# Attention on one core: the accumulator as two one-bank tiles, two second halves one place later, and copies of g and of the sums dealt anew between ScalarE and VectorE

## The chip, the cores and the metric

The kernel runs on one core of a Trainium2 chip. The metric is the device time of one execution in microseconds. Three runs of the kernel before took 578.69, 578.71 and 579.06 us; their median is 578.71 us.

A core has a matrix engine (TensorE, "PE" in the profile, with its weight loads as "PEld"), a vector engine (VectorE, "DVE"), a scalar engine (ScalarE, "ACT"), GpSimd ("POOL"), and a synchronisation engine (SyncE, "SP"). Each engine takes its instructions in the order in which the program issued them. Matmuls write to PSUM; here a PSUM bank is a tile of 128 partitions by 512 float32 columns. VectorE and ScalarE read PSUM and write to SBUF, where all operands of a matmul lie.

## The reference

Two graph layers work on x (16 batches, 1024 nodes, 64 channels) with one matrix adj (1024 x 1024). What matters here:

```
Q = x Wq^T + bq;  K = x Wk^T + bk;  V = x Wv^T
score = softmax(Q K^T, axis=1)           # over the first node index
x = layernorm(x + (score @ adj) @ V)     # adj is (1024, 1024) here too
# second layer: x, adj x, 2 adj (adj x) - x, for each of two equal supports,
# concatenated, times a weight, plus a bias
x = layernorm(x + that)
```

Everything is float32. The kernel computes Q K^T as x G x^T with one 64 x 64 matrix G (g2 in the code) and one bias vector gb. It keeps g = G x + gb, transposed (GT in the code), as one side of the scores, and the transposed x (xT) as the other.

## The kernel before

**Pairs and steps.** Two batches form a pair, one on partitions 0 to 63 and one on 64 to 127 of the transposed tiles. The loop at line 678 runs over pairs p = 0 to 7, and inside it over steps m = 0 to 7, one for each block of 128 nodes. A step computes the scores of the *next* step for both batches (j = 0 and 1) in two halves of 512 columns (h = 0 and 1), their maxima (`nm`, line 398, VectorE) and exponentials (`e`, line 400, ScalarE, which also yields the sums `es`). It then scales rows of U by the reciprocals of the sums (`scaled`, lines 403 to 413, giving `us`) and multiplies: `weighted` (line 415) adds us times e into the accumulator ACC[p], over all eight steps. In the code `weighted(p, m, t, h)` takes the node half t, which is a row half of TensorE, and the column half h. The part t = 0 runs in the step itself, t = 1 in the step after.

**Tiles of TensorE.** Every matmul of the loop uses 64 rows and 64 columns of the array, so four can run side by side. The program alternates between rows 0 to 63 (j = 0 or t = 0) and rows 64 to 127 (j = 1 or t = 1). A float32 matmul is issued twice, so each appears twice in the counts of the profile.

**Runs.** Beside the attention, U = adj x (first layer) and a product for the second layer are computed by a seven-product scheme in blocks, in pieces called runs (class Run, line 653). Each step carries one run, six steps two (`two_runs`, line 605). A run has four parts, part(t, i), and is then evicted from PSUM by VectorE by a small program of additions (`Hop.evict`, line 280): "u=" copies, "+p" adds the product to a destination, "u+p" to the tile u, and "+u" adds u to a destination, all in SBUF.

**Small products.** Some steps carry a small product as well (`small_of`, line 633). At m=1 it is `values` of the pair before, which multiplies the attended rows OT by the value weights and adds to x. At m=4 it is `project`, which makes GT for the next pair. At m = 7, 0, 2 and 3 it is `mix` of an earlier pair, which feeds the second layer. Each comes in two halves, j=0 and j=1, through one PSUM bank: the two run and small tiles f0 and f1 take turns, and a small product takes the bank that the last run left (`f_other`). The second half can only start when VectorE and ScalarE have taken the first out of the bank. In `project` (line 340) a half is copied to GT in two pieces b = 0 and 1, which lie on partitions 0 to 63 and 64 to 127 of the bank. Lines 359 to 362 deal the pieces: of the four copies ScalarE has three (line 366) and VectorE one (line 370), the second piece of the first half.

**End of a pair.** The first step of pair p (m=0) finishes the accumulator of pair q = p-1. After `weighted(..., 1, 0)`, `attended(q, 0)` copies its columns 0 to 511 to OT on ScalarE (line 437). After `weighted(..., 1, 1)`, `attended(q, 1)` copies columns 512 to 1023. ACC[p] is one tile of two banks (line 418) in a pool with one buffer.

**Order.** The schedule is written out by hand. Other VectorE work is attached to steps as jobs (`first_gap`, lines 607 to 631): sums for the runs, means and centring of x, a normalisation, transposes whose results go through DRAM by GpSimd's DMA queue, and weights of the second layer. They run after the first exponential of the step is issued. In steps with two runs the first run is evicted before the second maximum is taken (lines 738 to 745). After the loop, line 753 on, the second layer is finished; it begins with a tile `wide` in the accumulator's place (line 978). Ahead of the loop, the same place holds `pv` (line 571), evicted at once at line 577.

Of the kernel before, what the change touches and what calls it, by code (L numbers as in the profile page):

```python
# [26 lines left out]
def gnn_kernel(  # L27
# [126 lines left out]
    def mix_weights():  # L154
        nc.vector.tensor_add(w24, w1s[:, 2], w1s[:, 4])
        nc.vector.tensor_scalar(w3[:, 0], w24, 2.0, None, op0=ALU.mult)
        nc.vector.tensor_add(w3[:, 1], w1s[:, 1], w1s[:, 3])
        nc.vector.tensor_sub(w3[:, 2], w1s[:, 0], w24)
        for j in range(2):
            nc.vector.tensor_add(w3[half[j], 2], w3[half[j], 2], ident[half[j], half[j]])  # L160
# [72 lines left out]
    class Hop:  # L233
# [45 lines left out]

        def evict(self, po, n, group, copy=nc.vector.tensor_copy):  # L280
            po = po[:, 0 : len(group) * Q].rearrange("p (g q f) -> p g q f", q=2, f=P)
            u = self.u[:, group[0] : group[-1] + 1].rearrange("p g (q f) -> p g q f", q=2)
            for op in self.todo[n].split():
                if op == "u=":
                    copy(u, po)
                elif op == "u+p":
                    nc.vector.tensor_tensor(u, po, u, ALU.add)
                else:
                    d = self.d(int(op[0]), int(op[1]), group)
                    x, y = {"=": (po, u), "+p": (po, d), "+u": (u, d)}[op[2:]]  # L290
                    nc.vector.tensor_tensor(d, x, y, ALU.add)

# [10 lines left out]
    def by_place(t):  # L303
        return t.rearrange("c (a k n) -> c a k n", k=K8, a=A4)

    def rows(p):
# [33 lines left out]
    def project(p, js, pq):  # L340


        if 0 in js:
            GT[p] = att.tile([P, N], FP, tag="GT", name="GT")

        def made():
            for b in range(2):
                for j, t in zip(js, pq):
                    nc.tensor.matmul(  # L349
                        t[half[b]], g2[half[j], half[j]], xT(p)[half[j], ts(b, H)],  # L350
                        start=True, stop=True,
                    )

        def places(vector):
            for j, t in zip(js, pq):
                for b in range(2):


                    if vector == ((j, b) == (0, 1) if len(js) == 1 else j == 1):
                        g = by_block(GT[p])[half[j], 2 * b : 2 * b + 2]  # L360
                        q = t[half[b]].rearrange("c (a k n) -> c a k n", a=2, k=K8)
                        yield g, q, gb[half[b]]

        def by_scalar():
            for g, q, bias_ in places(False):
                nc.scalar.activation(g, q, AF.Identity, bias=bias_)

        def by_vector():
            for g, q, bias_ in places(True):
                nc.vector.tensor_scalar(g, q, bias_, None, op0=ALU.add)  # L370
        return (made,), by_scalar, by_vector
# [12 lines left out]
    def scores(sc, p, m, j, h):  # L384

        for c in range(2):
            nc.tensor.matmul(  # L387
                sc[half[c], ts(h, H)], GT[p][half[j], m * P + c * C : m * P + (c + 1) * C],
                xT(p)[half[j], ts(h, H)], start=True, stop=True,
            )  # L390

    def exps(p, m, j, sc):

        if j == 0:
            PU[p, m] = ([], small.tile([P, 2], FP, tag="es", name="es"))
        es, sm = PU[p, m]
        nm = small.tile([P, 1], FP, tag="nm", name="nm")
        nc.vector.tensor_reduce(nm, sc, AX.X, ALU.max, negate=True)  # L398
        e = att.tile([P, N], FP, tag="e", name="e", bufs=4)
        nc.scalar.activation(e, sc, AF.Exp, bias=nm, accum_out=sm[:, j : j + 1])  # L400
        es.append(e)
# [13 lines left out]
    def weighted(p, m, t, h):  # L415

        if (m, t, h) == (0, 0, 0):
            ACC[p] = pacc.tile([P, N], FP, tag="acc", name="acc")
        es, us = PU[p, m]
        made = [  # L420
            nc.tensor.matmul(  # L421
                ACC[p][half[j], ts(h, H)], us[half[t], j], es[j][half[t], ts(h, H)],
                start=m == 0 and t == 0, stop=m == K8 - 1, skip_group_check=True,
# [7 lines left out]

    def attended(p, h):

        if h == 0:
            OT[p] = att.tile([P, N], FP, tag="oT", name="oT", bufs=1)
        a = slice(2 * h, 2 * h + 2)
        nc.scalar.activation(by_block(OT[p])[:, a], by_place(ACC[p])[:, a], AF.Copy)  # L437

    def values(p, js, po):


        def made(ks):
            for k in ks:
                for t in range(2):
                    for j, o in zip(js, po):
                        n = k * P + t * C
                        nc.tensor.matmul(  # L447
# [122 lines left out]
    sums_of_adj(3)  # L570
    pv = pacc.tile([P, N], FP, tag="acc", name="pv")
    hop_0.product(pv, 4, (0, 1), False)
    for do in both(project, 0):
        do()
    sums_of_adj(2)
    hop_0.product(pv[:, H:], 4, (2, 3), False)
    hop_0.evict(pv, 4, ALL)
    sc = [sc_tile(f"sc{j}") for j in range(2)]
# [3 lines left out]
    for j in range(2):  # L582
        exps(0, 0, j, sc[j])

# [27 lines left out]
    at(second_gap, (0, 0), lambda: transposed(1, xT(1)))  # L612
    at(first_gap, (0, 1), sums_of_adj, 1)
    at(first_gap, (0, 2), sums_of_adj, 4)
    at(first_gap, (0, 3), mix_weights)
    at(first_gap, (0, 4), value_weights)
    for step, n in ((1, 0), 1), ((2, 0), 2), ((2, 5), 3), ((3, 0), 4):
        at(first_gap, step, hop_1.sums, n)
    at(first_gap, (1, 0), centred, w3)
    for step, n in ((HP + 1, 5), 1), ((HP + 2, 0), 2), ((HP + 2, 7), 3), ((NP - 1, 0), 4):  # L620
        at(first_gap, step, hop_z.sums, n)
    for p in range(NP):

        at(first_gap, {2: (2, 1), 6: (4, 5)}.get(p, (p, 5)), means, p)
        at(first_gap, {6: (5, 6)}.get(p, (p, 6)), centre, p)
        if p + 1 < NP:
# [12 lines left out]
    SYNC = mybir.DependencyInfo(mybir.DependencyClass.Sync, mybir.DependencyReason.DATA)  # L639
    sum_mark = []  # L640

    def passed(made):
# [10 lines left out]
    class Run:  # L653
# [13 lines left out]
        def evict(self):  # L667
            self.hop.evict(self.po[:, 0:Q], self.n, self.group)

# [6 lines left out]
    late = [whole_run() for _ in range(2)]  # L676
    tail, before = None, None
    for p in range(NP):
        q = p - 1
        for m in range(K8):  # L680
# [3 lines left out]
            sc = sc_tile("sc0")  # L684
            scores(sc, *nxt, 0, 0)
            if tail:
                tail.part(1, 1)
                tail.evict()
            scores(sc, *nxt, 0, 1)
# [11 lines left out]
            if before:  # L701
                weighted(*before, 1, 1)
                if m == 0:
                    attended(q, 1)
                PU.pop(before)
            todo[0].part(0, 0)
            what = small_of.get((p, m))
            sc1 = sc_tile("sc1")
            if what:
# [3 lines left out]
            if what:  # L713
                for do in parts[1:]:
                    do()
                by_scalar()
            else:
                todo[0].part(0, 1)
            exps(*nxt, 0, sc)
            if m == 6 and p:  # L720
                x0T_in_order(q)
            if what:
                by_vector()
            for do in first_gap.get((p, m), ()):
                do()
# [3 lines left out]
            elif len(todo) > 1:  # L729
                todo[1].part(0, 0)  # L730
                todo[1].part(0, 1)
                todo[0].part(1, 0)
            weighted(p, m, 0, 0)
            if what:
                parts, by_scalar, by_vector = what[0](*what[1:], (1,), [f_other("small1")])
                parts[0]()
                by_scalar()
            if len(todo) > 1:
                todo[0].part(1, 1)
                todo[0].evict()  # L740
            weighted(p, m, 0, 1)
            if what:
                for do in parts[1:]:
                    do()
            exps(*nxt, 1, sc1)
            if what:
                by_vector()
            todo[-1].part(1, 0)
            for do in second_gap.get((p, m), ()):
# [3 lines left out]
    tail.part(1, 1)  # L753
    tail.evict()
    scaled(NP - 1, K8 - 1)
    for h in range(2):
        weighted(*before, 1, h)
    evict = whole_run()
    es, us = PU.pop((NP - 1, K8 - 1))
    for h in range(2):  # L760
        for j in range(2):
            made = nc.tensor.matmul(
                ACC[NP - 1][half[j], ts(h, H)], us[:, j], es[j][:, ts(h, H)],
                start=False, stop=True, skip_group_check=True,
# [203 lines left out]
    def add_w(c, i):  # L968
# [8 lines left out]
    w = [pw.tile([P, H], FP, tag="w", name=f"w{i}") for i in range(4)]  # L977
    wide = pacc.tile([P, N], FP, tag="acc", name="wide")
    held.update({
        (1, 0): wide[:, 0:H], (1, 1): wide[:, H:], (2, 0): w[0], (2, 1): w[3],  # L980
        (5, 0): w[1], (5, 1): w[0], (7, 0): w[3], (7, 1): w[2],
# [206 lines left out]
```

## Time and profile before

| | |
|---|---|
| median of three runs | 578.71 us |
| profiled execution, its own time | 578.6 us |
| its span in the profile | 576.8 us |
| loop over the pairs, in the trace | about 32 to 422 us |
| weighted sums, L421 PE | 1008 matmuls, 240.1 us busy |
| scores, L387 PE | 1024 matmuls, 241.8 us busy |
| maxima, L398 DVE | 128, mean 1217 ns |
| exponentials, L400 ACT | 128, mean 1114 ns |
| copies of the sums, L437 ACT | 16, mean 597 ns |
| copies of g, small tiles: L366 ACT, L370 DVE | 21 of mean 682 ns, 7 of mean 755 ns |
| granted TensorE clock | 0.993 |

A row of the profile names the line, the engine and the operation, what is written and from what, and how often; then the busy time and the mean of one, and the idle time just before such instructions with what ended it. Busy times of matmuls overlap, so they add up to more than the span. In the timeline each row has a start, a length and a count of instructions merged into it, and in brackets the idle time ahead of it with its releaser.

### The profile page before, as it was taken

How to read it: one execution, taken by the hardware profiler on the slowest of the kernel's cores; microseconds unless marked ns; L12 is line 12 of the kernel's file. 1: busy time of each engine (PE TensorE's matmuls, PEld its weight loads, DVE VectorE, ACT ScalarE, POOL GpSimd, SP SyncE). 2: the span in 40 equal slices, each digit the busy share in tenths (PEclk: the TensorE clock that was granted, in tenths of full speed). 3: DMA queues.
4: the chain of work that ended last, by engine and by line, in shares of the span. 5: the costliest groups of instructions: out<-in, count | busy, mean ns of one | idle time of the engine just before them, and what ended most of it. 6: DMA issues, size and time to landing. Idle time of an engine off the chain costs nothing.

```text
span 576.8 us, 14499 instructions
## 1 busy us (share of the span) xinstructions
PE 558.9 (97%) x6150; PEld 398.2 (69%) x6150; DVE 438.2 (76%) x710; ACT 254.8 (44%) x532; POOL 153.0 (27%) x145
## 2 busy tenths in 40 slices
PE   9999999999999999999999999999999999999992
PEld 7757567666756766765676676567678789888552
DVE  0788887877887887788788888888847575799784
ACT  1133544555656556564654556555522300041561
POOL 0001001211211202021121102102102895693784
PEclk9999999999999999999999999999999999999997
DMA  8902001022022012101202010100201400002943
GB/s 274 323 3 74 2 38 39 1 75 74 3 74 76 1 39 74 39 23 54 75 1 76 37 39 22 54 2 2 75 2 62 86 0 1 2 18 51 206 145 92
DMA packets 20994, 33.66 MB, mean 58 GB/s; under 512 B 3010, under 2 KB 12482, under 8 KB 20546
## 3 DMA queue, kind: packets, MB, share of 16 engines
q0 software_dynamic: 6880, 18.88, 11.3%
q1 hardware_dynamic: 14050, 13.86, 7.3%
q8 instruction: 48, 0.79, 0.6%
q14 instruction: 16, 0.13, 0.1%
HBM read 16.48 MB, written 12.06 MB: 49 GB/s over the span
## 4 chain that ended last, share of the span: by engine, by line
PE 85%; DVE 6%; ACT 3%; DMA 2%; issue 1%; SPq 0%; POOL 0%; POOLq 0%; ACTq 0%; DVEq 0%
PE p L266 19%; PE sc L387 18%; PE acc L421 15%; PE w L795 14%; PE small L500 4%; PE w L1103 3%; PE wide L795 2%; DVE nm L398 2%; PE pu L256 2%; PE small L349 2%; PE small L447 2%; ACT e L400 2%; PE pv L256 1%; PE p L256 1%; DMA aT<-in_adjT_dram 1%
## 5 line engine op out<-in xcount | busy, mean ns | idle before, releaser
L421 PE MATMUL acc<-e,us 64*64 64x512 f32 x1008 | 240.1, 591 | 5.3 <-ACT oT L437 5.3
L387 PE MATMUL sc<-xT,GT 64*64 64x512 f32 x1024 | 241.8, 594 | 0.3 <-ACT e L400 0.3
L400 ACT ACTIVATE e<-sc,nm 128x1024 f32<-128x1024 f32 x128 | 142.6, 1114 | 123.2 <-DVE nm L398 105.4
L398 DVE TENSOR_REDUCE nm<-sc 128x1 f32<-128x1024 f32 x128 | 155.8, 1217 | 3.4 <-PE sc L387 3.0
L421 PEld LDWEIGHTS acc<-e,us 64*64 64x64 f32 x1008 | 69.2, 133 | 36.4 <-ACT oT L437 11.5
L466 POOL TENSOR_TENSOR rstd<-var,expo 128x16 f32<-128x16 f32 (+3 forms) x21 | 50.9, 2428 | 140.4 <-DVE var L464 140.3
L387 PEld LDWEIGHTS sc<-xT,GT 64*64 64x64 f32 x1024 | 66.7, 132 | 13.9 <-ACT e L400 5.5
L333 POOL DMA_DIRECT2D d<-blocks x14 | 8.4, 597 | 196.6 <-DVE blocks L328 196.6
L266 PE MATMUL p<-UY,aT 64*64 64x256 f32 x480 | 59.3, 377 | 0.0
L266 PE MATMUL p<-XB,S 64*64 64x256 f32 x480 | 58.6, 377 | 0.0
L266 PE MATMUL p<-UY,S 64*64 64x256 f32 x384 | 46.3, 377 | 0.0
L266 PE MATMUL p<-XB,aT 64*64 64x256 f32 x352 | 43.6, 378 | 0.0
L266 PEld LDWEIGHTS p<-XB,S 64*64 64x64 f32 x480 | 32.7, 133 | 13.9 <-issue 5.4
L266 PEld LDWEIGHTS p<-UY,aT 64*64 64x64 f32 x480 | 33.0, 133 | 12.5 <-issue 3.2
L500 PE MATMUL small<-w,x0T_k 64*64 64x192 f32 x384 | 39.5, 323 | 0.0
L500 PEld LDWEIGHTS small<-w,x0T_k 64*64 64x64 f32 x384 | 26.5, 133 | 10.1 <-issue 3.5
L266 PEld LDWEIGHTS p<-UY,S 64*64 64x64 f32 x384 | 26.0, 133 | 10.2 <-issue 2.8
L266 PE MATMUL p<-xs,aT 64*64 64x256 f32 x256 | 31.3, 377 | 0.0
L266 PE MATMUL p<-xs,S 64*64 64x256 f32 x256 | 31.2, 377 | 0.0
L266 PEld LDWEIGHTS p<-XB,aT 64*64 64x64 f32 x352 | 23.9, 133 | 9.5 <-issue 3.5
L808 ACT COPY own<-w 128x512 f32<-128x512 f32 x8 | 4.5, 587 | 54.6 <-PE w L795 54.6
L510 ACT ACTIVATE UY<-small 128x128 f32<-128x128 f32 x48 | 13.3, 278 | 31.0 <-PE small L500 30.1
(210 smaller groups left out, 942.5 us busy)
## 6 DMA issues: line engine op xcount, KB each, us to landing
d<-blocks POOLq DMA_DIRECT2D x14, 512.0 KB, 3.0
xs<-own POOLq DMA_DIRECT2D x8, 512.0 KB, 6.5
xT<-d POOLq DMA_DIRECT2D x28, 128.0 KB, 2.9
x0T<-d POOLq DMA_DIRECT2D x28, 128.0 KB, 2.9
out_dram<-xs SPq DMA_DIRECT2D x14, 256.0 KB, 2.2
xs<-in_x_dram SPq DMA_DIRECT2D x3, 1024.0 KB, 7.7
aT<-in_adjT_dram SPq DMA_DIRECT2D x8, 256.0 KB, 4.9
aT<-in_adjT_dram SPq DMA_DIRECT2D x4, 512.0 KB, 8.9
```

The source lines that it names most:

```text
L256: nc.tensor.matmul(po[t * w : (t + 1) * w], SIDE[n][:, k, j : j + w], self.side[n][:, :, k, :], start=start, stop=True, skip_group_check=True,
L266: nc.tensor.matmul(po[half[c]], SIDE[n][half[t], k, i * P + c * C : i * P + (c + 1) * C], self.side[n][half[t], :, k, :], start=t == 0 and ...
L349: nc.tensor.matmul(t[half[b]], g2[half[j], half[j]], xT(p)[half[j], ts(b, H)], start=True, stop=True,)
L387: nc.tensor.matmul(sc[half[c], ts(h, H)], GT[p][half[j], m * P + c * C : m * P + (c + 1) * C], xT(p)[half[j], ts(h, H)], start=True, stop= ...
L398: nc.vector.tensor_reduce(nm, sc, AX.X, ALU.max, negate=True)
L400: nc.scalar.activation(e, sc, AF.Exp, bias=nm, accum_out=sm[:, j : j + 1])
L421: nc.tensor.matmul(ACC[p][half[j], ts(h, H)], us[half[t], j], es[j][half[t], ts(h, H)], start=m == 0 and t == 0, stop=m == K8 - 1, skip_gr ...
L466: nc.gpsimd.tensor_tensor(rstd, var, expo[:, 0:n], ALU.pow)
L500: nc.tensor.matmul(t[half[c], 0:3, k], X0T[p][half[j], n : n + C], w3[half[j]], start=True, stop=True,)
L510: nc.scalar.activation(part(UY, j), t[:, 0], AF.Copy)
L795: nc.tensor.matmul(po[:, ts(g, b.shape[1] * P)], a[:, k, ts(g, P)], b[:, :, k, :], start=start and g == 0 and k == 0, stop=True, skip_grou ...
L1103: nc.tensor.matmul(po, SIDE[n][:, k, ts(i, P)], B_F[n][:, k, cols], start=k == 0, stop=k == K4 - 1)
```

## The change

The accumulator becomes two tiles of one bank each, ACC[p, 0] and ACC[p, 1], for its two column halves; `pv` before the loop and `wide` behind it are split in the same way, and pv is evicted in two pieces. GT and OT are stored with the node order of a half contiguous (`half_block`, `half_place`), where the pieces of both halves were interleaved before; the matmuls that read them take other columns of the same data.

The second halves of `values` and `project` come one place later: after the second part of the weighted sum, with the run's `part(1, 0)` in their old place. For `values`, the last products and VectorE's addition are kept (`pending`) until after the first score of the next step. `mix` stays where it was.

The copies of g are dealt so that VectorE takes piece b = 1 of both halves. In a projection step its first copy is issued after the step's jobs. The copy of the accumulator's second half at m=0 is issued after the first maximum, and goes to VectorE in pairs 1, 4 and 5 (`sums_at_0`). A maximum is now an instruction of its own (`maximum`): the second of a step is issued before VectorE evicts the first of two runs. Of an eviction, the additions "+u" are split off and issued after the first maximum and the jobs. Some jobs move: part of the mix weights from step (0,3) to (0,5), the means of pair 0 from (0,5) to (0,6), its centring from (0,6) to (1,0), the first sum of hop_1 from (1,0) to (1,1), and the centring of w3 from (1,0) to (1,3).

```diff
-                    if vector == ((j, b) == (0, 1) if len(js) == 1 else j == 1):
-                        g = by_block(GT[p])[half[j], 2 * b : 2 * b + 2]
-                        q = t[half[b]].rearrange("c (a k n) -> c a k n", a=2, k=K8)
-                        yield g, q, gb[half[b]]
+                    if vector == (b == 1 if len(js) == 1 else j == 1):
+                        yield half_block(GT[p][half[j]], b), half_place(t[half[b]]), gb[half[b]]
...
+    def maximum(sc):
+        nm = small.tile([P, 1], FP, tag="nm", name="nm")
+        nc.vector.tensor_reduce(nm, sc, AX.X, ALU.max, negate=True)
+        return nm
...
-        if (m, t, h) == (0, 0, 0):
-            ACC[p] = pacc.tile([P, N], FP, tag="acc", name="acc")
+        if m == 0 and t == 0:
+            ACC[p, h] = pacc.tile([P, H], FP, tag=f"acc{h}", name="acc")
...
-    def attended(p, h):
+    def attended(p, h, vector=False):
 
         if h == 0:
             OT[p] = att.tile([P, N], FP, tag="oT", name="oT", bufs=1)
-        a = slice(2 * h, 2 * h + 2)
-        nc.scalar.activation(by_block(OT[p])[:, a], by_place(ACC[p])[:, a], AF.Copy)
+        src = half_place(ACC.pop((p, h)))
+        if vector:
+            nc.vector.tensor_copy(half_block(OT[p], h), src)
+        else:
+            nc.scalar.activation(half_block(OT[p], h), src, AF.Copy)
...
+    sums_at_0 = {(p, 0) for p in range(1, NP) if p not in (2, 3, HP + 2, NP - 1)}
...
+            for do in pending:
+                do()
+            pending, rest = [], []
             if tail:
                 tail.part(1, 1)
-                tail.evict()
+                rest = tail.evict()
...
             if before:
                 weighted(*before, 1, 1)
-                if m == 0:
-                    attended(q, 1)
                 PU.pop(before)
...
-                by_scalar()
             else:
                 todo[0].part(0, 1)
-            exps(*nxt, 0, sc)
+            nm = maximum(sc)
+            if m == 0 and before:
+                attended(q, 1, (p, m) in sums_at_0)
+            if what:
+                by_scalar()
+            exps(*nxt, 0, sc, nm)
...
+            jobs = first_gap.get((p, m), []) + rest
             if what:
-                by_vector()
-            for do in first_gap.get((p, m), ()):
+                jobs.insert(len(jobs) if what[0] is project else 0, by_vector)
+            for do in jobs:
                 do()
...
+            nm = maximum(sc1)
             weighted(p, m, 0, 0)
-            if what:
+            if soon:
                 parts, by_scalar, by_vector = what[0](*what[1:], (1,), [f_other("small1")])
                 parts[0]()
                 by_scalar()
-            if len(todo) > 1:
+                exps(*nxt, 1, sc1, nm)
+                by_vector()
+            elif what:
+                todo[0].part(1, 0)
+            elif len(todo) > 1:
                 todo[0].part(1, 1)
-                todo[0].evict()
+                exps(*nxt, 1, sc1, nm)
+                rest = todo[0].evict()
+                for do in rest:
+                    do()
+            else:
+                exps(*nxt, 1, sc1, nm)
             weighted(p, m, 0, 1)
-            if what:
-                for do in parts[1:]:
-                    do()
-            exps(*nxt, 1, sc1)
-            if what:
-                by_vector()
-            todo[-1].part(1, 0)
+            if what and not soon:
+                parts, by_scalar, by_vector = what[0](*what[1:], (1,), [f_other("small1")])
+                parts[0]()
+                pending = [*parts[1:], by_vector]
+                by_scalar()
+                if not pending[1:]:
+                    pending.pop()()
+                exps(*nxt, 1, sc1, nm)
+            else:
+                todo[-1].part(1, 0)
```

Here `soon` is true where the small product is `mix`, and `tail.evict()` returns the additions "+u" that were split off.

More of the change, by code (lines that the diff above doesn't have):

```diff
@@ L157, in mix_weights, with more_mix_weights @@
         nc.vector.tensor_add(w3[:, 1], w1s[:, 1], w1s[:, 3])
+    def more_mix_weights():
         nc.vector.tensor_sub(w3[:, 2], w1s[:, 0], w24)
@@ L280, in evict, with evictions @@
         def evict(self, po, n, group, copy=nc.vector.tensor_copy):
+            for do in self.evictions(po, n, group, copy):
+                do()
+        def evictions(self, po, n, group, copy=nc.vector.tensor_copy):
+            rest = []
             po = po[:, 0 : len(group) * Q].rearrange("p (g q f) -> p g q f", q=2, f=P)
@@ L290, in evict @@
                     x, y = {"=": (po, u), "+p": (po, d), "+u": (u, d)}[op[2:]]
-                    nc.vector.tensor_tensor(d, x, y, ALU.add)
+                    do = lambda d=d, x=x, y=y: nc.vector.tensor_tensor(d, x, y, ALU.add)
+                    rest.append(do) if x is u else do()
+            return rest
     A4 = P // 32
@@ L304, in by_place, with half_block, half_place @@
         return t.rearrange("c (a k n) -> c a k n", k=K8, a=A4)
+    def half_block(t, h):
+        return t[:, ts(h, H)].rearrange("c (k b n) -> c b k n", k=K8, b=2)
+    def half_place(t):
+        return t.rearrange("c (b k n) -> c b k n", b=2, k=K8)
     def rows(p):
@@ L387, in scores, with exps @@
             nc.tensor.matmul(
-                sc[half[c], ts(h, H)], GT[p][half[j], m * P + c * C : m * P + (c + 1) * C],
+                sc[half[c], ts(h, H)], GT[p][half[j], c * H + m * C : c * H + (m + 1) * C],
                 xT(p)[half[j], ts(h, H)], start=True, stop=True,
             )
-    def exps(p, m, j, sc):
+    def maximum(sc):
+        nm = small.tile([P, 1], FP, tag="nm", name="nm")
+        nc.vector.tensor_reduce(nm, sc, AX.X, ALU.max, negate=True)
+        return nm
+    def exps(p, m, j, sc, nm):
         if j == 0:
@@ L396, in exps @@
         es, sm = PU[p, m]
-        nm = small.tile([P, 1], FP, tag="nm", name="nm")
-        nc.vector.tensor_reduce(nm, sc, AX.X, ALU.max, negate=True)
         e = att.tile([P, N], FP, tag="e", name="e", bufs=4)
@@ L421, in weighted @@
             nc.tensor.matmul(
-                ACC[p][half[j], ts(h, H)], us[half[t], j], es[j][half[t], ts(h, H)],
+                ACC[p, h][half[j]], us[half[t], j], es[j][half[t], ts(h, H)],
                 start=m == 0 and t == 0, stop=m == K8 - 1, skip_group_check=True,
@@ L445, in made @@
                     for j, o in zip(js, po):
-                        n = k * P + t * C
+                        n = t * H + k * C
                         nc.tensor.matmul(
@@ L570, in gnn_kernel @@
     sums_of_adj(3)
-    pv = pacc.tile([P, N], FP, tag="acc", name="pv")
-    hop_0.product(pv, 4, (0, 1), False)
+    pv = [pacc.tile([P, H], FP, tag=f"acc{h}", name="pv") for h in range(2)]
+    hop_0.product(pv[0], 4, (0, 1), False)
     for do in both(project, 0):
@@ L575, in gnn_kernel @@
     sums_of_adj(2)
-    hop_0.product(pv[:, H:], 4, (2, 3), False)
-    hop_0.evict(pv, 4, ALL)
+    hop_0.product(pv[1], 4, (2, 3), False)
+    for h in range(2):
+        hop_0.evict(pv[h], 4, (2 * h, 2 * h + 1))
     sc = [sc_tile(f"sc{j}") for j in range(2)]
@@ L582, in gnn_kernel @@
     for j in range(2):
-        exps(0, 0, j, sc[j])
+        exps(0, 0, j, sc[j], maximum(sc[j]))
     y = [[quarter(UY, 0, r, c) for c in range(2)] for r in range(2)]
@@ L612, in gnn_kernel @@
     at(second_gap, (0, 0), lambda: transposed(1, xT(1)))
[L613 to L617, printed above, removed]
+    for step, do in (
+        ((0, 1), lambda: sums_of_adj(1)), ((0, 2), lambda: sums_of_adj(4)), ((0, 3), mix_weights),
+        ((0, 4), value_weights), ((0, 5), more_mix_weights), ((1, 3), lambda: centred(w3)),
+    ):
+        at(first_gap, step, do)
+    for step, n in ((1, 1), 1), ((2, 0), 2), ((2, 5), 3), ((3, 0), 4):
         at(first_gap, step, hop_1.sums, n)
-    at(first_gap, (1, 0), centred, w3)
     for step, n in ((HP + 1, 5), 1), ((HP + 2, 0), 2), ((HP + 2, 7), 3), ((NP - 1, 0), 4):
@@ L622, in gnn_kernel @@
     for p in range(NP):
-        at(first_gap, {2: (2, 1), 6: (4, 5)}.get(p, (p, 5)), means, p)
-        at(first_gap, {6: (5, 6)}.get(p, (p, 6)), centre, p)
+        at(first_gap, {0: (0, 6), 2: (2, 1), 6: (4, 5)}.get(p, (p, 5)), means, p)
+        at(first_gap, {0: (1, 0), 6: (5, 6)}.get(p, (p, 6)), centre, p)
         if p + 1 < NP:
@@ L667, in evict @@
         def evict(self):
-            self.hop.evict(self.po[:, 0:Q], self.n, self.group)
+            return self.hop.evictions(self.po[:, 0:Q], self.n, self.group)
     def whole_run():
@@ L677, in gnn_kernel @@
     tail, before = None, None
+    pending = []
     for p in range(NP):
@@ L707, in gnn_kernel @@
             what = small_of.get((p, m))
+            soon = what and what[0] is mix
             sc1 = sc_tile("sc1")
@@ L737, in gnn_kernel @@
                 by_scalar()
-            if len(todo) > 1:
-                todo[0].part(1, 1)
-                todo[0].evict()
-            weighted(p, m, 0, 1)
-            if what:
-                for do in parts[1:]:
-                    do()
-            exps(*nxt, 1, sc1)
-            if what:
-                by_vector()
-            todo[-1].part(1, 0)
+                exps(*nxt, 1, sc1, nm)
[3 more added lines that the diff above has]
+            elif len(todo) > 1:
+                todo[0].part(1, 1)
+                exps(*nxt, 1, sc1, nm)
+                rest = todo[0].evict()
+                for do in rest:
+                    do()
+            else:
+                exps(*nxt, 1, sc1, nm)
+            weighted(p, m, 0, 1)
+            if what and not soon:
[8 more added lines that the diff above has]
+                todo[-1].part(1, 0)
             for do in second_gap.get((p, m), ()):
@@ L753, in gnn_kernel @@
     tail.part(1, 1)
-    tail.evict()
+    rest = tail.evict()
     scaled(NP - 1, K8 - 1)
+    for do in rest:
+        do()
     for h in range(2):
@@ L762, in gnn_kernel @@
             made = nc.tensor.matmul(
-                ACC[NP - 1][half[j], ts(h, H)], us[:, j], es[j][:, ts(h, H)],
+                ACC[NP - 1, h][half[j]], us[:, j], es[j][:, ts(h, H)],
                 start=False, stop=True, skip_group_check=True,
@@ L977, in gnn_kernel @@
     w = [pw.tile([P, H], FP, tag="w", name=f"w{i}") for i in range(4)]
-    wide = pacc.tile([P, N], FP, tag="acc", name="wide")
+    wide = [pacc.tile([P, H], FP, tag=f"acc{h}", name="wide") for h in range(2)]
     held.update({
-        (1, 0): wide[:, 0:H], (1, 1): wide[:, H:], (2, 0): w[0], (2, 1): w[3],
+        (1, 0): wide[0], (1, 1): wide[1], (2, 0): w[0], (2, 1): w[3],
         (5, 0): w[1], (5, 1): w[0], (7, 0): w[3], (7, 1): w[2],
```

## The prediction

> **What bounds the kernel.** I read the page's head first, then the waits of TensorE, then windows cut at the steps of one pair, then the timeline inside the steps that lose time.
>
> ```profile
> span 576.8 us, 14499 instructions
> PE 558.9 (97%) x6150; PEld 398.2 (69%) x6150; DVE 438.2 (76%) x710; ACT 254.8 (44%) x532; POOL 153.0 (27%) x145
> ```
>
> TensorE is at 97% and no other engine is near. But a matmul here uses a quarter of the array, 64 rows by 64 columns, and the busy share counts a moment as busy when only one row half works. So I count work. On one tile, 512-column issues follow each other every 0.43 us (179.49, 179.92 below). A step needs on each row half four of them for scores, four for the weighted sum, and eight of 256 columns for its run: 12 x 0.43 = 5.12 us. A mix adds four of 192 columns (0.16 us apart), 5.76; a values or a projection step adds 0.85, 5.97. Windows from the first score of a step to that of the next, for pair 3 (time: length, then busy times by engine):
>
> ```profile
> 178.63:185.50 6.87, 6.11 (x87) 4.17 (x80) 5.10 (x10) 4.39 (x10) 2.59 (x5) 1.00 0.44 151
> 185.50:191.59 6.09, 6.09 (x130) 4.56 (x124) 5.13 (x9) 2.41 (x4) 0.00 (x0) 1.00 0.02 4
> ...
> 203.22:209.34 6.12, 6.12 (x77) 3.71 (x71) 4.68 (x8) 3.35 (x7) 0.00 (x0) 1.00 0.00 0
> 209.34:215.23 5.89, 5.89 (x77) 3.42 (x71) 4.92 (x8) 3.77 (x6) 0.61 (x1) 1.00 0.24 92
> ...
> sum 47.68, PE 46.92 PEld 32.18 DVE 38.83 ACT 27.85 POOL 8.46; mean PE 5.87 PEld 4.02 DVE 4.85 ACT 3.48 POOL 1.06
> ```
>
> Needed: 5.76, 5.97, 5.76, 5.76, 5.97, 5.12, 5.12, 5.76, together 45.22. Taken: 47.68. Of the 2.46 us lost, 1.11 lie in step m=0, 0.12 in m=1 (values), 0.15 in m=4 (projection), 0.77 in m=5 just behind it, 0.31 in the rest. The same counting over pairs 0 to 7 gives some 20 us in all; the rest of the loop is TensorE's own work, which the change leaves alone. The waits name the causes (engine, line, what for: total us, times, longest):
>
> ```profile
> PE acc L421 <- ACT oT L437: 5.3, 7, 0.8
> PEld acc L421 <- ACT oT L437: 11.5, 7, 1.7
> PEld sc L387 <- ACT e L400: 5.5, 16, 0.7
> PEld small L349 <- DVE GT L370: 5.1, 7, 0.7
> PEld small L447 <- DVE xs L455: 2.3, 7, 0.4
> ```
>
> **The accumulator's two tiles.** The timeline of TensorE, then ScalarE, at m=0 of pair 3:
>
> ```profile
> 179.49 0.60 PE L387 MATMUL sc<-xT,GT 64*64 64x512 f32 x2
> ...
> 179.99 0.60 PE L421 MATMUL acc<-e,us 64*64 64x512 f32 x2
> 181.34 0.65 PE L421 MATMUL acc<-e,us 64*64 64x512 f32 x2 [0.76 <-ACT oT L437]
> 181.35 0.65 PE L266 MATMUL p<-XB,aT 64*64 64x256 f32 x4
> ```
> ```profile
> 179.39 1.11 ACT L400 ACTIVATE e<-sc,nm 128x1024 f32<-128x1024 f32 x1 [0.89 <-DVE nm L398]
> 180.40 0.19 ACT L400 ACTIVATION_READ_ACCUMULATOR e<-sc,nm 128x1 f32 x1
> 180.69 0.60 ACT L437 ACTIVATE oT<-acc 128x512 f32<-128x512 f32 x1
> ```
>
> The matmul at 181.34 fills columns 512 to 1023 of acc. It waits for the copy of columns 0 to 511, which ends at 181.29 and queued behind an exponential. It needs none of that data: the wait comes from both halves being one tile. TensorE issues in order, so the run behind it (181.35) waits too. The tile was free at 179.99 + 0.43 = 180.42, so 0.92 us stand still on both row halves. Seven such places (m=0 of pairs 1 to 7) show 0.92 to 0.94; 7 x 0.93 = 6.5 us. What is late next, with everything moved up 0.92: the small product needs the last run's eviction (ends 180.53; TensorE is there at 181.2), the second score tile needs the exponential (180.59; 181.3), the new pair's accumulation needs the first copy (181.29; 182.7). All have 0.6 us or more to spare. The second small product needs its bank read by ScalarE and VectorE, near 182.9, and comes at 183.0: tight. I take 6.5, with 3 as the lower end.
>
> **Values half one place later.** At m=1 the second small product (190.33) waited 0.23 us behind VectorE's addition (0.69 us, L455), with rows 64 to 127 idle since 190.09. Now the run's part goes there first. Only one row half stood still: between 0 and 7 x 0.23 = 1.6, I take 0.5. The deferred addition now stands ahead of the next eviction on VectorE, where the next run's bank is needed only some 0.6 us after it is free.
>
> **The projection.** VectorE and ScalarE at m=4 and m=5 of pair 3:
>
> ```profile
> 207.60 0.76 DVE L370 TENSOR_SCALAR GT<-small,gb 64x512 f32<-64x512 f32 x1 [0.67 <-ACT GT L366]
> 208.39 1.25 DVE L328 STREAM_TRANSPOSE blocks<-xs 128x1024 f32<-128x1024 f32 x1
> ```
> ```profile
> 206.89 0.68 ACT L366 ACTIVATE GT<-small,gb 64x512 f32<-64x512 f32 x1 [1.61 <-PE small L349]
> ...
> 209.54 1.38 ACT L366 ACTIVATE GT<-small,gb 64x512 f32<-64x512 f32 x2 [0.88 <-PE acc L421]
> 210.99 1.11 ACT L400 ACTIVATE e<-sc,nm 128x1024 f32<-128x1024 f32 x1
> ```
>
> Before, the second product waited for VectorE's copy (208.36) and ran at 208.41, 0.32 after rows 64 to 127 fell idle. After, VectorE transposes first and copies g at 208.2 to 208.95; the run's part fills that time, and the product goes at 209.0, ending 209.85. Its copies: ScalarE 210.05 to 210.73, then VectorE 0.76 more. Here a rule meets a row. The Trainium skill's page "PSUM — Partial Sum Buffer", section "PSUM bank collisions raise a hardware error", says that two engines clash on a bank only within the same 32 partitions. The two halves of a small product lie on partitions 0 to 63 and 64 to 127, so by the rule both could be read at once, ending 210.8, before the next run needs the bank at 210.93: 0.5 us more per pair, 3.5 in all. The row shows VectorE idle 0.67 us until ScalarE's copy is done: the program orders the whole bank. I follow the row: the bank is free at 211.5, and the run starts 0.6 late on rows 0 to 63, later than its 211.11 of before. Its second part was held until 212.26 anyway, so 0.2 is given back there; the first score of m=6, which waited for an exponential (215.23), comes between 0.2 earlier and, where VectorE has two evictions of 0.42 in this chain, 0.15 later. Per pair -0.2 to +0.5, I take +0.1: 0.7 over seven pairs. A second rule, page "ScalarE: Activation LUTs", section "Rules for kernel authors", wants additions on VectorE. Here the copy with its bias takes 0.682 on ScalarE and 0.755 on VectorE: the seven copies dealt anew gain 0 by the row, and I count no gain for the cheaper engine.
>
> **Maxima first, sums later.** In the six steps with two runs, the second maximum stood behind two evictions (0.76). At m=6 of pair 4 the score at 270.43 waits for an exponential whose chain starts there; TensorE had been free since 270.10: 0.33. The same wait is 0.34 at m=3 of pair 0. With the later additions "+u" (0.42 each) moved behind the maximum, some five such places gain 0.2 each: 1.0, between 0 and 2.
>
> **Moved VectorE work** issues no DMA of its own: three mix weights (0.65) move from m=3 to m=5 of pair 0, means and centring (1.21 each) one place on, sums of hop_1 (1.22) from m=0 to m=1 of pair 1, centring of w3 (0.70) to m=3, where it joins a normalisation and VectorE has about 5.5 us of work for a 5.1 us step. VectorE has slack elsewhere; I take -0.1, between -0.6 and +0.3. The transpose ahead of g issues its five GpSimd transfers 0.8 earlier; nothing queues for them. The first eviction of pv becomes two of 0.69 for one of 1.23, its first half under a matmul stream: 0. Three copies of acc on VectorE (about 0.75 by L370's row; ScalarE 0.60) sit ahead of the small bank's release, 0.35 late on one row half: -0.1 each, -0.3; if covered, nothing.
>
> **Sum:** 6.5 + 0.5 + 0.7 + 1.0 - 0.1 - 0.3 = 8.3. The span would go from 576.8 to 568.5. The profiled run took 578.6, 1.8 beside its span, and the median is 578.7: 570.4.
>
> **Rivals.** *Everything small goes too* (20%): copies of g side by side, 0.5 in seven pairs, plus the ends of the other terms: 6.5 + 1.2 + 3.5 + 1.5 = 12.7, 566.0. For it: the new g layout no longer interleaves the halves in SBUF, so an order that came from there would vanish. Against: L515 also waits for ScalarE (8.4 us over 48) and shares only the bank. *A new wait in place of the old* (13%): the small bank or the second score tile stops TensorE half as long, 3.3 + 1.7 = 5.0, 573.7. For: both are needed within 0.1 to 0.7 us; against: what releases them moves up as well. *The halves still wait* (4%), the copy tied to the tile's owner in another way: only the 1.8 of the rest, 576.9. *Slower* (6%): VectorE's second copy of g, behind a maximum and the bank's order, holds the next run, and its 0.6 adds to the 0.8 by which eviction, maximum and exponential follow: 1.4 us in each of seven projection steps, 9.8 against 8.3, 580.2. It decides from 1.2 us per pair on; against it, rows 64 to 127 still have 1.7 us of weighted sums queued ahead.
>
> The forecast itself has 57%. The range leaves out the last two cases and the tail of the first rival: 566.4 to 574.2; the forecast's own range is 568.5 to 572.5. A difference under 0.2% (1.2 us) can't be told from none; half of the "still wait" case falls there. Faster 0.91, same 0.03, slower 0.06.
>
> **What would show it.** Right: no row of acc waiting for oT; m=0 windows near 5.8 to 5.9 us; small L447 no longer waiting for xs. L366 with about 14 copies and L370 with 14, the latter still idle behind ScalarE. Wrong: L370 starting beside L366; a new wait of p at m=5 for GT; m=0 still over 6.3.

## The result and the profile after

The changed kernel took 571.6 us in the median of four runs (571.51 to 572.14), against 578.7 us for the kernel before beside it: a ratio of 0.9878, with a 95% interval of 0.9861 to 0.9895. The forecast was 570.4 us. The profiled run is the highest of the four, 572.1 us; its loop over the pairs began 0.57 us later than in the profile before (36.27 against 35.70 us), since TensorE waited longer for the first blocks of adj. Seven of the kernels below run the same code ahead of the loop and began it between 35.4 and 36.1 us, a second profile of the changed kernel at 36.5, so this start varies by itself and is not counted for the change.

The head of the page, and then all waits of TensorE's matmuls of 0.3 us or more in total (engine, line, what for: total us, times, longest):

```profile
span 570.4 us, 14498 instructions
PE 557.4 (98%) x6150; PEld 404.6 (71%) x6150; DVE 443.1 (78%) x721; ACT 248.6 (44%) x522; POOL 153.2 (27%) x145
```
```profile
PE idle L128 <- DVE g L87: 1.1, 1, 1.1
PE pu L258 <- DMA aT<-in_adjT_dram: 0.9, 2, 0.6
PE small L367 <- DVE GT L385: 0.3, 1, 0.3
```

The seven waits of acc for oT, 5.3 us before, are gone. Among the weight loads, the two waits of small products for VectorE that were quoted in the prediction have shrunk or gone as well, but one row has grown from 1.0 us (4 times) to this:

```profile
PEld p L268 <- SPq L667: 9.4, 26, 0.6
PEld small L367 <- DVE GT L385: 0.8, 1, 0.8
```

The windows of pair 3, step by step as in the prediction (time: length, then busy times):

```profile
177.13:182.94 5.81, 5.81 (x86) 4.37 (x80) 5.09 (x10) 4.38 (x10) 2.61 (x5) 1.00 0.38 138
182.94:189.05 6.11, 6.11 (x112) 4.24 (x103) 5.13 (x9) 2.41 (x4) 0.00 (x0) 1.00 0.14 44
189.05:195.20 6.15, 6.15 (x110) 4.72 (x108) 4.70 (x10) 4.21 (x9) 0.18 (x1) 1.00 0.01 3
...
201.01:207.03 6.02, 6.02 (x79) 4.04 (x74) 5.21 (x9) 3.13 (x6) 0.61 (x1) 1.00 0.00 0
207.03:213.03 6.00, 6.00 (x74) 3.59 (x70) 5.02 (x8) 3.09 (x5) 2.19 (x4) 1.00 0.48 168
```

Step m=0 fell from 6.87 to 5.81 us. But m=2 rose from 5.82 to 6.15, and m=5 from 5.89 to 6.00, while PE is busy in every moment of every window: at any time at least one row half works, and the loss lies in the other. So I count as the prediction did: the length of each step less the work that one row half has in it, summed over the 62 whole steps of the loop. These are the microseconds lost, by m, for five of the kernels below:

| step | before | changed | tiles alone (e1) | values early (e3) | both early (f1) |
|---|---|---|---|---|---|
| m=0 | 8.10 | 0.45 | 0.50 | 0.45 | 0.45 |
| m=1 (values) | 0.96 | 1.22 | 0.96 | 1.25 | 1.62 |
| m=2 | 0.83 | 2.77 | 0.80 | 0.62 | 0.63 |
| m=3 | 1.14 | 0.64 | 1.14 | 0.64 | 0.64 |
| m=4 (project) | 1.27 | 0.85 | 1.27 | 1.81 | 1.41 |
| m=5 | 5.08 | 6.33 | 5.08 | 6.73 | 4.90 |
| m=6 | 1.81 | 0.35 | 1.80 | 0.35 | 0.58 |
| m=7 | 0.66 | 0.44 | 0.66 | 0.44 | 0.49 |
| sum | 19.86 | 13.06 | 12.20 | 12.29 | 10.74 |

The change won 7.65 us at m=0 and 2.2 at m=3, 6 and 7, and gave back 2.2 at m=1 and 2 and 0.8 at m=4 and 5.

The work of a step is set a little too low in this count. The prediction's 12 x 0.43 is 5.16, not 5.12: in the trace 512-column issues follow each other every 0.429 us and 256-column issues every 0.216. So about 0.04 us of every step, some 2.5 us of every sum, is no loss. The differences between the columns are not touched.

### The profile page after: what moved, and what is told of

Its sections match the earlier page's. It is cut to its first block, busy times and chain, and to the rows that moved or that the text cites. A ratio compares the mean times of both kernels' runs of the same rounds, so it can differ in the third digit from the quotient of the medians.

```text
span 570.4 us, 14498 instructions
## 1 busy us (share of the span) xinstructions
PE 557.4 (98%) x6150; PEld 404.6 (71%) x6150; DVE 443.1 (78%) x721; ACT 248.6 (44%) x522; POOL 153.2 (27%) x145
## 4 chain that ended last, share of the span: by engine, by line
PE 88%; DVE 5%; DMA 2%; ACT 2%; SPq 1%; issue 1%; POOL 0%; POOLq 0%; ACTq 0%; DVEq 0%
PE p L268 20%; PE acc L439 18%; PE sc L402 18%; PE w L841 14%; PE small L521 3%; PE w L1149 3%; PE wide L841 2%; PE small L468 2%; PE pu L258 2%; PE pv L258 1%; DVE nm L409 1%; PE small L367 1%; DMA aT<-in_adjT_dram 1%; PE p L258 1%; PE both L521 1%; ACT e L418 1%
## 5 line engine op out<-in xcount | busy, mean ns | idle before, releaser
L439 PE MATMUL acc<-e,us 64*64 64x512 f32 x1008 | 237.3, 589 | 0.0
```

What stands on the lines that cost most here:

```text
L439: nc.tensor.matmul(ACC[p, h][half[j]], us[half[t], j], es[j][half[t], ts(h, H)], start=m == 0 and t == 0, stop=m == K8 - 1, skip_group_che ...
```

## The experiments

Each kernel was timed against the kernel before on the same chip (578.7 to 578.9 us). **Theory A**: the two tiles carry the whole gain; the reordered small products cost, and what else was reordered pays that back. **Theory B**: the parts need each other.

**e1, the tiles alone.** The kernel before, with this and the same split of pv and wide:

```diff
-        if (m, t, h) == (0, 0, 0):
-            ACC[p] = pacc.tile([P, N], FP, tag="acc", name="acc")
+        if m == 0 and t == 0:
+            ACC[p, h] = pacc.tile([P, H], FP, tag=f"acc{h}", name="acc")
```

> The kernel before with the accumulator, pv and wide in one-bank tiles and nothing else. Theory A (the tiles carry the whole gain, the rest of the change sums to nothing): the seven stalls of 0.93 us at m=0 go, and as the windows of the changed kernel lost 7.65 us less in all eight m=0 steps, the time is 571.2 to 572.0. Rival B (the freed time needs the reordering around it, since the second small product's bank was released only 0.1 us before it was wanted): 573.5 to 575.

Measured: 571.17 us (ratio 0.9867, 0.9852 to 0.9881), at the lower edge of A's range and as fast as the changed kernel, whose interval overlaps this one. The table shows that only m=0 differs from before.

**e2, one tile again**, the rest of the change kept:

```diff
-            ACC[p, h] = pacc.tile([P, H], FP, tag=f"acc{h}", name="acc")
+            whole = pacc.tile([P, N], FP, tag="acc", name="acc")
+            for i in range(2):
+                ACC[p, i] = whole[:, ts(i, H)]
```

> The changed kernel with the accumulator, pv and wide as one tile of two banks again, read in halves by the new patterns. Theory A: the wait of acc for oT is back at seven places and the time is 578 to 580. Rival B (the new order around it does part of the work): 575 to 577. Rival C (not the tile but the old four-block read pattern made the two halves look overlapping): no wait of acc for oT, 571.5.

Measured: 579.34 us (ratio 1.0008, 1.0 to 1.0017), in A's range. The waits of TensorE in this kernel:

```profile
PE acc L441 <- ACT oT L460: 5.8, 7, 1.2
PE idle L128 <- DVE g L87: 1.1, 1, 1.1
```

The wait is back at its seven places, though the halves are now read by the new, plainly separate patterns: it hangs on the tile. Together e1 and e2 show that the rest of the change sums to nothing, within 0.5 us.

**e3, the second half of values at its old place**, project still late:

```diff
+            early = what and what[0] is values
...
-            if soon:
+            if soon or early:
                 parts, by_scalar, by_vector = what[0](*what[1:], (1,), [f_other("small1")])
                 parts[0]()
...
-                by_vector()
+                if soon:
+                    by_vector()
...
             weighted(p, m, 0, 1)
-            if what and not soon:
+            if early:
+                for do in parts[1:]:
+                    do()
+                by_vector()
+            if what and not soon and not early:
```

> The changed kernel with the second half of values at its old place (product right after the first half of the weighted sum, addition before the next step); project stays late. Theory A (moving values late costs: m=2 windows lose 0.39 instead of 0.05 because the next run waits for a bank that VectorE frees late, and m=1 has a 0.36 us wait for the ordering mark of the run): 569.3 to 570.2, m=2 back at 0.05. Rival (the old 0.23 us wait of values for VectorE comes back in full, on both row halves): 571.2 to 572.

Measured: 570.89 us (ratio 0.9862, 0.9846 to 0.9878), 0.7 to 0.8 below the changed kernel: neither range was met, and the sign is A's. The loss at m=2 went as A had it, from 2.77 to 0.62, but m=4 and m=5 gave back 1.4 of that. At m=4 of pair 3, for instance, rows 0 to 63 stand for 0.11 us in e3 behind the run's part on the other rows (205.10 to 205.21); in the changed kernel, where they come later against the other rows, not at all. So the losses of values and of project in part overlap.

**h1, values late but not kept** for the next step:

```diff
-                if not pending[1:]:
-                    pending.pop()()
+                for do in pending:
+                    do()
+                pending = []
```

> The changed kernel, with the second half of values late but not kept for the next step: its last products and VectorE's addition are issued at the end of the step. Theory A (of the 0.34 us lost at m=2, 0.2 or more is the next run's wait for the bank that the kept addition frees late; the addition now comes some 0.9 us sooner): m=2 loses 0.05 to 0.2, the time is 569.6 to 570.6. Rival (it is the wait of the run's part for its ordering mark at m=1 that surfaces at m=2): m=2 still loses 0.35 to 0.4, 571.2 to 571.9.

Measured: 571.61 us, beside 571.67 for the changed kernel itself (g0). In pair 3, m=2 lost 0.10 instead of 0.39, as A said, but m=1 lost 0.60 instead of 0.14. So A had the loss at m=2 and not the time; the rival had the time and not the loss. A's wait for the bank is there. VectorE and TensorE of the changed kernel at m=2 of pair 3:

```profile
190.31 0.69 DVE L476 TENSOR_TENSOR xs<-small,xs 128x512 f32<-128x512 f32 x1 [1.33 <-PE small L468]
```
```profile
190.39 0.59 PE L402 MATMUL sc<-xT,GT 64*64 64x512 f32 x1
...
191.06 0.65 PE L268 MATMUL p<-XB,aT 64*64 64x256 f32 x4
```

Rows 0 to 63 are free at 190.39 + 0.43 = 190.82; the run starts at 191.06, just behind the kept addition (190.31 + 0.69 = 191.00), 0.24 us late. In h1 the run follows its score without a gap, but the first score of m=2 now stands for 0.48 us behind the products of values (last section). So h1 put one block in the place of another, and does not tell how much the bank is worth by itself.

The weight loads of the changed kernel where values are put late, and of e3:

```profile
187.11 0.36 PEld L439 LDWEIGHTS acc<-e,us 64*64 64x64 f32 x4
187.90 0.14 PEld L268 LDWEIGHTS p<-XB,aT 64*64 64x64 f32 x2 [0.43 <-SPq L667]
```
```profile
186.39 0.35 PEld L439 LDWEIGHTS acc<-e,us 64*64 64x64 f32 x4
187.05 0.43 PEld L468 LDWEIGHTS small<-wv,oT 64*64 64x64 f32 x12 [0.31 <-DVE xs L476]
```

In the first, the run's part(1, 0) fills the gap. It adds to the bank in which part(0, 1) has just worked with the other row half, and a mark, an instruction on SyncE that waits for the one and is waited for by the other, keeps the two apart. Rows 64 to 127 fall idle at 187.54 (the last score starts at 187.11 and takes 0.43) and start again at 187.90: 0.36 us. In e3 values waits for VectorE instead: idle at 186.82, on again at 187.05, 0.23 us. The move swapped a hole of 0.23 us for one of 0.36, and put values last, in front of the next step's first score. In h1, where its rest stands ahead of that score, the loss shows at m=1, in the changed kernel at m=2. How the loss divides between the mark, the bank and the order is not shown by these runs.

**e4, project at its old place**, new dealing of g, VectorE's first copy behind the job, values late. The edit is e3's with `project` for `values`, and VectorE's copy is issued right behind the second exponential, as for `mix`.

> The changed kernel with the second half of project at its old place; the dealing of g stays new (VectorE has the second piece of each half, the first behind the step's jobs); values stay late. Theory A (with the first piece of g copied only behind the transposition, the second product would stop TensorE some 0.9 us): 573.5 to 577. Rival (placing it late is worth nothing by itself, as m=4 and m=5 together lose 0.93 us against 0.92 before): 571.2 to 572.2.

Measured: 573.88 us (ratio 0.9913, 0.9898 to 0.9928). A's range was met. TensorE stands before the second product until VectorE, behind a transposition of 1.2 us, has made its first copy:

```profile
PE small L367 <- DVE GT L385: 2.8, 6, 1.1
```

**Four ways of project**, all with values early. f3 is e3 with VectorE's first copy ahead of the step's job; f4 is f3 with project early; f1 is f4 with the old dealing; f2 is f1 with project late. Against e3, the first edit below is in f1 and f2, the second in f1 and f4, the third in all four.

```diff
-                    if vector == (b == 1 if len(js) == 1 else j == 1):
+                    if vector == ((j, b) == (0, 1) if len(js) == 1 else j == 1):
...
-            early = what and what[0] is values
+            early = what and what[0] in (values, project)
...
-                jobs.insert(len(jobs) if what[0] is project else 0, by_vector)
+                jobs.insert(0, by_vector)
```

> The changed kernel with values and project as before the change (second halves at the old place, old dealing of g, VectorE's copy of g ahead of the step's jobs); the accumulator's tiles, maxima first, additions later, moved jobs and sums on VectorE stay. Theory A (each reordered small product costs time: m=4 and m=5 of the run with values early lost 8.54 us over the loop where the kernel before lost 6.35): 568.4 to 569.3, faster than either kernel. Rival (the steps around need the new project: the time is given back at m=5 and m=6): 570.5 to 571.5.

> As the last one, but the second half of project late (its new place) with the old dealing, where ScalarE makes both copies of the second half. Theory A (the exponential of the second scores waits for two copies of 0.68 us that start later, so that the next maximum and exponential come later too): 571.5 to 574. Rival (the new dealing on VectorE is what costs, by holding the bank and VectorE's queue): 568.5 to 570.

> The changed kernel with values early (as in e3_values_early) and VectorE's first copy of g ahead of the step's jobs; project late, new dealing. Theory A (the second copy waits for ScalarE's, which the order of the first does not move): 570.5 to 571.2, as e3_values_early. Rival (the copy behind the transposition holds the second product): 569.3 to 570.2.

> As f1_all_early_old_deal, but with the new dealing of g (VectorE has the second piece of each half, the first ahead of the jobs). Theory A (ScalarE and VectorE read the same bank one after the other, so the dealing frees nothing, and the second copy stands behind a maximum that is itself late): 569.0 to 570.5. Rival (ScalarE's exponential 0.68 us earlier shortens m=5): 567.0 to 568.3.

| project's second half | old dealing | new dealing |
|---|---|---|
| old place | f1: 569.56 | f4: 569.49 |
| new place | f2: 574.26 | f3: 570.86 |

All four went A's way, f1 and f2 just above its ranges. At the old place the dealing changes nothing (0.07 us). The new place costs 4.7 us with the old dealing and 1.4 with the new: the dealing is a repair of the place. f3 equals e3 (570.89), so with the product late the place of the first copy makes no difference.

In f2 ScalarE's two copies start later and push the second exponential behind them; in the changed kernel one of them is VectorE's. The first block is f2, the second the changed kernel, both ScalarE at m=4 of pair 3:

```profile
208.12 1.38 ACT L381 ACTIVATE GT<-small,gb 64x512 f32<-64x512 f32 x2 [1.78 <-PE small L367]
209.52 1.11 ACT L418 ACTIVATE e<-sc,nm 128x1024 f32<-128x1024 f32 x1
```
```profile
208.01 0.68 ACT L381 ACTIVATE GT<-small,gb 64x512 f32<-64x512 f32 x1 [1.57 <-PE small L367]
208.72 1.11 ACT L418 ACTIVATE e<-sc,nm 128x1024 f32<-128x1024 f32 x1
```

**g0 and g1: the changed kernel and f1 side by side:**

> The changed kernel as it is, to be timed beside the two others on the same chip: 571.2 to 571.9.

> The kernel of f1_all_early_old_deal (values and project as before the change, the rest of the change kept), to be timed beside the changed kernel. Theory A: 569.1 to 569.9, 0.3 to 0.4% below the changed kernel. Rival: the two overlap.

Measured: 571.67 us (571.23 to 572.52; ratio to before 0.9879, 0.9865 to 0.9892) and 569.53 us (569.42 to 569.81; 0.9841, 0.9827 to 0.9854). Their runs don't overlap: f1's program, with the tiles, the maxima first and the moved jobs but values and project as they were, is 2.1 us faster than the changed kernel and beats both.

## Why the prediction was right, and which terms were not

The direction, the mechanism of the main term and the total held: 8.3 us were forecast and 7.1 measured. Term by term the sum was less good, and that the total came so near was in part luck: the tiles and the reordered maxima brought some 2 us more than forecast, values and project some 3 us less. One of the prediction's own signs of being wrong came true as well, a run at m=5 that waits for GT.

**The accumulator: 6.5 forecast, 7.7 measured** (e1 against before; 7.65 in the windows). The wait went and nothing took its place, by the margins that were worked out. The mis-sized term is the 0.93 us of standstill per place: the windows quoted with it had 1.11 lost at m=0, and now lose 0.05. The other 0.13 also belonged to the stop, after which the next three issues on rows 64 to 127 came 0.48, 0.46 and 0.48 us apart (181.34, 181.82, 182.28, 182.76) instead of 0.43.

**Values: +0.5 forecast, a loss measured**: 2.2 us in the windows of m=1 and 2, of which 0.7 to 0.8 shows in the time. The step that failed is "now the run's part goes there first", costed as if it were free to go. I had checked the bank it leaves, not the mark it waits for. The list of waits had a row for runs waiting on SyncE (1.0 us, 4 times) that I passed over as small; a part moved forward by one place of 0.85 us meets its mark. The margin that I saw at the deferred addition, some 0.6 us before the next run needs its bank, was not there either: the run came 0.24 us late.

**Project: +0.7 forecast, 0.8 lost** in the windows of m=4 and 5, and 1.3 to 1.4 us in time (f3 against f1 and f4). Here the working held: the row against the rule was the right choice. VectorE, then TensorE, at m=5 of pair 3 of the changed kernel:

```profile
208.72 0.76 DVE L385 TENSOR_SCALAR GT<-small,gb 64x512 f32<-64x512 f32 x1 [0.90 <-ACT GT L381]
209.51 0.42 DVE L299 TENSOR_TENSOR UY<-p,UY 128x256 f32<-128x256 f32 x1
```
```profile
208.32 0.60 PE L402 MATMUL sc<-xT,GT 64*64 64x512 f32 x2
...
209.54 0.65 PE L268 MATMUL p<-XB,aT 64*64 64x256 f32 x4
```

VectorE idles 0.90 us, until ScalarE is done with the same bank, and its copy ends at 209.48. The run (209.54) needs that bank and could have started at 208.75: 0.79 us on rows 0 to 63, forecast as 0.6. I weighed this against a gain at the exponential and took +0.1 per pair from a range of -0.2 to +0.5; the measured -0.12 in the windows and -0.2 in time are inside it. A part that I missed is again the mark, 0.36 us at m=4. No run read both halves of a bank at once, so what the Trainium skill's page "PSUM — Partial Sum Buffer" says of different partitions stays untested: the program orders the whole bank. The second rule weighed, additions on VectorE, did not hold here: 683 ns on ScalarE against 756 on VectorE over 14 copies each. The page "ScalarE: Activation LUTs" gives a speed in bf16 as its reason; these copies are float32.

**Maxima first and additions later: 1.0 forecast, 1.4 to 1.6 measured** (e1 against f1, each beside its own runs of the kernel before or in plain difference; 2.2 in the windows of m=3, 6 and 7). The moved jobs and the sums on VectorE are in it, so the forecast to compare is 1.0 - 0.1 - 0.3 = 0.6, and no run takes these apart. The largest single place is m=6 of pair 4, where I read only the 0.33 us before one score. The maxima of its exponential, VectorE, before and after:

```profile
264.19 0.43 DVE L291 TENSOR_TENSOR UY<-p,UY 128x256 f32<-128x256 f32 x1 [0.32 <-PE p L266]
264.53 0.41 DVE L287 TENSOR_TENSOR u<-p,u 128x256 f32<-128x256 f32 x1
264.87 1.21 DVE L398 TENSOR_REDUCE nm<-sc 128x1 f32<-128x1024 f32 x1
```
```profile
260.65 1.21 DVE L409 TENSOR_REDUCE nm<-sc 128x1 f32<-128x1024 f32 x1
261.78 0.41 DVE L299 TENSOR_TENSOR UY<-p,UY 128x256 f32<-128x256 f32 x1
262.11 0.41 DVE L295 TENSOR_TENSOR u<-p,u 128x256 f32<-128x256 f32 x1
```

With the maximum ahead of the two evictions, the step fell from 6.05 to 5.16 us. In the changed kernel m=5 of the same pair lost 0.45 more, but that is project's: in f1, with project as before, m=6 is as short and m=5 as before.

**Sums on VectorE: -0.3 forecast, nothing measured.** Pairs 1, 4 and 5 lose the same at m=0 as the others (0.05 to 0.06), the copy taking 0.68 us there against 0.60 on ScalarE.

Of the rivals, "everything small goes too" failed at the bank, as the row said; "a new wait" came true in other steps than it named, behind values and project, for some 2 us (0.8 and 1.3) in place of the 3.3 it put on m=0; "the halves still wait" and "slower" did not occur.

## What to carry to other kernels

Where an engine that issues in order is shared by two interleaved streams, a wait that has no data behind it stops both: split the tile on which it hangs, and the gain is the length of the step less its work, not only the idle time in the row. Before an instruction is moved into a hole, list what *it* waits for, ordering marks included, and not only what it frees. And take a change apart once it has won: here one part carried it all, and two others could be undone at a profit.

## What the runs showed of the hardware that was not expected

The ordering mark between two row halves waited for more than the part that it orders. TensorE of the changed kernel at m=1 of pair 3, ahead of the weight load at 187.90 that is shown with h1:

```profile
187.11 0.38 PE L268 MATMUL p<-XB,aT 64*64 64x256 f32 x1
187.11 0.59 PE L402 MATMUL sc<-xT,GT 64*64 64x512 f32 x1
```

The part ahead of the mark ends at 187.49 (ends of matmuls are modelled), 0.41 us before that weight load, the first behind the mark; at m=4 of pair 3 it is 0.54 (205.48 to 206.02), in e3 0.74 (204.44 to 205.18). So the part's end does not set the time. The score that the program issues just before the part, on rows 64 to 127, ends at 187.70, 205.83 and 204.99: 0.19 us before the weight load each time, and 0.19 at all 14 places of values and project in the changed kernel. SyncE's own instruction takes 17 ns of it. So the mark passed when that score was done, on the very rows that then waited, and these ran empty: the 0.36 us. That it counts the score together with the part fits these times; no run moved the score away.

And rows 0 to 63 could be held by work that they have no part in. TensorE in h1, at the end of m=1 of pair 3:

```profile
188.07 0.59 PE L439 MATMUL acc<-e,us 64*64 64x512 f32 x2
188.27 0.92 PE L468 MATMUL small<-wv,oT 64*64 64x64 f32 x26
188.98 0.65 PE L402 MATMUL sc<-xT,GT 64*64 64x512 f32 x2
```

Rows 0 to 63 are free at 188.07 + 0.43 = 188.50, and the operands of the first score of m=2 are there, but it stands in the program behind the values of rows 64 to 127 and starts at 188.98, 0.48 us later.
